# A cross-attention block on one core: scores leave PSUM two heads at a time, most maxima are finished on VectorE, and the order of all engines is written anew

## The chip, the cores and the metric

The kernel runs on one core of a Trainium2 chip. The metric is the device time of one launch in microseconds (us); lower is better. The core has five engines with queues of their own: TensorE (PE, matmuls), VectorE (DVE), ScalarE (ACT), GpSimd (POOL) and SyncE (SP, which here only issues DMAs). Each takes its instructions in order and waits for the others by semaphores. TensorE writes its results to PSUM, which has eight banks of 128 partitions x 512 fp32 numbers; the other data lie in SBUF.

## The reference

Eight batches of 256 tokens, width 512, 16 heads of 32, all in fp32:

```python
def layer_norm(x, w, b):
    mu = jnp.mean(x, axis=-1, keepdims=True)
    var = jnp.mean(jnp.square(x - mu), axis=-1, keepdims=True)
    return (x - mu) * jax.lax.rsqrt(var + EPS) * w + b
x = layer_norm(hidden_states, ln1_w, ln1_b)
q = (x @ q_w + q_b).reshape(B, LQ, H, HD).transpose(0, 2, 1, 3)
k = (encoder_hidden_states @ k_w + k_b).reshape(B, LK, H, HD).transpose(0, 2, 1, 3)
v = (encoder_hidden_states @ v_w + v_b).reshape(B, LK, H, HD).transpose(0, 2, 1, 3)
scores = jnp.einsum('bhqd,bhkd->bhqk', q, k) * scale
scores = jnp.where(mask, scores, mask_value)
attn = jax.nn.softmax(scores, axis=-1)
out = jnp.einsum('bhqk,bhkd->bhqd', attn, v)
out = out @ cproj_w + cproj_b
hidden = out + residual
y = layer_norm(hidden, ln2_w, ln2_b)
y = jax.nn.gelu(y @ fc_w + fc_b, approximate=True)
y = y @ proj_w + proj_b
return residual + y
```

The MLP's inner width is 2048. Queries and keys are 256 tokens each.

## The kernel before, in words

**Stages.** The eight batches are worked in two groups of four (g = 0, 1). For each group: the context and the normalised tokens are turned (transposed) by TensorE or VectorE; q, k and v are projected; 16 attention units follow (four heads hg by batch b, named u = g, hg, b: unit 132 is group 1, heads hg = 3, batch 2); then the output projection with the residual (o), LayerNorm, the MLP's first product (fc) with gelu, and its second (pd). Group 0's attention lies beside group 1's projections, group 1's attention beside the output projection and the first fc products.

**Projections** use Strassen's scheme in Winograd's form: a product of 2 x 2 blocks takes seven matmul groups P1 to P7 instead of eight, with sums of blocks before (names ending in s, t, i such as `fw0i`, `z1t`, `a0t`, made on VectorE or GpSimd) and after (the evictions `t1` to `t3`, `c11` to `c22`). fc and pd use it on two levels. X, Y and W name the banks that such a product holds.

**One attention unit.** Eight score matmuls (L1023; each matmul leaves two records in the profile) put keys by queries into four banks, one head a bank, two key blocks each. ScalarE moves each head and key block to SBUF, adding the mask as a bias (`ev`, L614, 128x256, eight a unit). VectorE reduces with a 32x32 transpose to maxima over 32 x 32 blocks (`mx`, L1033, two a unit). ScalarE copies three 32x64 pieces of these from partitions 32, 64 and 96 to partition 0 (`mc`, L1039); VectorE reduces over the four pieces and the two key blocks (`fold`, L1040) and transposes once (`mf`, L1042). The result goes through DRAM and comes back broadcast over all partitions (`md`, `mm`), and is subtracted from the scores (`less`, L1053 on VectorE or L1057 on GpSimd), which then go through exp (L1060). `av`: TensorE multiplies the exponentials with v, and with ones for the sums of each row; `r` and `att` (L1083 to L1086, L625) divide. Of a unit of kind "z" the two key blocks are first added (`ss`, L625), and the row sums take four matmuls; of kind "p" they are not, and take eight. `KINDS` lists the kinds.

**What sets the order.** Each piece of work is one operation with a name (`T.op`). The table `PROGRAM` lists all names in one order; an operation that can run on several engines has a letter behind its name (:A ScalarE, :V VectorE, :G GpSimd). Each engine gets its operations in that order and no scheduler changes it. The table `PLACES` gives each buffer its slot of SBUF or its PSUM bank. The framework adds the semaphore waits that follow from it. The eight banks are eight tiles of 128x512, of kind W (projections) or C (scores, av, turns). A matmul waits until the last reader of the bank's previous contents is done.

**The start.** TensorE runs 12 small matmuls on constants first (`small`, L646), and 4 more behind the first turned blocks.

## Time and profile before

| | us |
|---|---|
| median of 3 runs (lowest, highest) | 654.15 (653.59, 655.86) |
| span of the profiled execution | 652.0 |
| TensorE busy in it | 644.3 |
| VectorE / ScalarE / GpSimd busy | 583.2 / 346.1 / 395.9 |
| start of the scores of unit 000; of 031; of 100 (group 1's first) | 63.2; 158.6; 186.4 |
| first product of group 1's output projection | 367.3 |
| last matmul's end | 648.5 |

The profile is one execution; its span lies 2.15 us below the median of the runs. In the rows an operation's line is that of the helper that records it (L634 is every matmul of the projections and of attention, L614 the score evictions, L601 and L606 other evictions, L623 and L625 sums). A row's tile names are those of the tile that was first put in the slot by that name in the program, so a projection may read "xt" or "vw" where another buffer has since taken that slot.

### The profile page before, as it was taken

The page shows a single profiled execution, that of the slowest core. Times are in us where ns is not written, and L with a number is a line of the kernel's source. Part 1 is how long each engine was busy: PE and PEld are TensorE (multiplying, and loading weights), DVE is VectorE, ACT ScalarE, POOL GpSimd, SP SyncE. Part 2 cuts the span into 40 slices and gives each one's busy share as a digit, 9 for nine tenths or more (in the row PEclk, how much of TensorE's full clock was granted, in tenths as well). Part 3 has the DMA queues.
Part 4 walks back from the last instruction along what each step waited for, and adds up shares of the span by engine and source line. Part 5 has one row for each costly group of instructions (what it writes and reads, how often), then busy time and mean ns, then how long its engine had stood idle before and what let it go on. Part 6 is the DMA issues. An engine that isn't in the chain of part 4 may idle for free.

```text
span 652.0 us, 11225 instructions
## 1 busy us (share of the span) xinstructions
PE 644.3 (99%) x3793; PEld 487.7 (75%) x3793; DVE 583.2 (89%) x985; ACT 346.1 (53%) x709; POOL 395.9 (61%) x351
## 2 busy tenths in 40 slices
PE   9999999999999999999999999999999999999997
PEld 7755463477545776777787888888888888888886
DVE  4989998999999999999999999988878777999975
ACT  2244698999999879966864645220121222523000
POOL 2543675879987897898859756335813265321244
PEclk9999999999999999999999999999999999999999
DMA  8999998778875447787867787897989989677765
GB/s 268 306 328 324 239 251 284 226 204 152 217 224 151 130 168 232 260 267 250 257 214 250 225 272 232 293 314 170 160 222 197 215 198 204 158 190 227 173 138 97
DMA packets 206713, 144.83 MB, mean 222 GB/s; under 512 B 117136, under 2 KB 167104, under 8 KB 206656
## 3 DMA queue, kind: packets, MB, share of 16 engines
q1 hardware_dynamic: 206656, 144.11, 78.0%
q8 instruction: 30, 0.49, 0.3%
q14 instruction: 27, 0.22, 0.1%
HBM read 104.10 MB, written 39.98 MB: 221 GB/s over the span
## 4 chain that ended last, share of the span: by engine, by line
PE 90%; DVE 4%; ACT 2%; issue 1%; DMA 1%; POOL 1%; DVEq 0%
PE pd_X L634 15%; PE fc_X L634 15%; PE fc_W L634 7%; PE pd_W L634 7%; PE av L634 6%; PE q_X L634 4%; PE v_X L634 4%; PE fc_Y L634 4%; PE k_X L634 4%; PE pd_Y L634 4%; PE s L634 4%; PE o_X L634 2%; PE v_W L634 2%; PE k_W L634 2%; PE o_W L634 2%; DVE mx L1033 2%
## 5 line engine op out<-in xcount | busy, mean ns | idle before, releaser
L614 ACT ACTIVATE pr<-s,cols 128x256 f32<-128x256 f32 x256 | 102.9, 485 | 10.7 <-PE s L634 8.2
L1057 POOL TENSOR_TENSOR pr<-pr,mm 128x512 f32<-128x512 f32 x70 | 90.2, 1318 | 7.2 <-DMA xt<-in_x_dram 5.0
L1237 ACT ACTIVATE h<-h,cols 128x256 f32<-128x256 f32 x128 | 55.2, 499 | 61.2 <-DVE h L625 45.2
L1033 DVE TRANSPOSE_TENSOR_REDUCE mx<-pr 128x32 f32<-128x1024 f32 x64 | 76.9, 1216 | 1.5 <-ACT pr L614 1.3
L1060 ACT ACTIVATE pr<-pr 128x1024 f32<-128x1024 f32 x64 | 66.5, 1061 | 12.1 <-POOL pr L1057 9.0
L625 DVE TENSOR_TENSOR h<-fc_X,h 128x512 f32<-128x512 f32 x80 | 52.4, 675 | 5.5 <-PE fc_X L634 4.7
L625 POOL TENSOR_TENSOR ss<-pr 128x512 f32<-128x512 f32 x24 | 31.5, 1325 | 14.2 <-ACT pr L1060 11.8
L625 DVE TENSOR_TENSOR h<-fc_W,h 128x512 f32<-128x512 f32 x48 | 32.0, 677 | 5.0 <-PE fc_W L634 4.4
L1053 DVE TENSOR_TENSOR pr<-pr,mm 128x1024 f32<-128x1024 f32 x29 | 35.2, 1229 | 0.0
L1039 ACT COPY mx<-mx 32x64 f32<-32x64 f32 x96 | 23.2, 243 | 15.9 <-DVE mx L1033 14.7
L623 POOL TENSOR_TENSOR z1t<-h,z1t 128x512 f32<-128x512 f32 x6 | 8.0, 1360 | 26.1 <-PE pd_Y L634 12.3
L625 POOL TENSOR_TENSOR tq<-tq,rq 128x512 f32<-128x512 f32 x8 | 10.1, 1272 | 21.7 <-DMA rq<-hd 15.4
L634 PE MATMUL pd_X<-z0i,pl 128*128 128x256 f32 x96 | 22.5, 379 | 0.0
L634 PE MATMUL fc_W<-y1i,fl 128*128 128x256 f32 x84 | 20.7, 379 | 0.0
L625 DVE TENSOR_TENSOR h<-fc_Y,h 128x512 f32<-128x512 f32 x24 | 15.9, 672 | 5.3 <-PE fc_Y L634 5.3
L634 PE MATMUL pd_W<-z1i,pl 128*128 128x256 f32 x88 | 20.6, 379 | 0.0
L1040 DVE TENSOR_REDUCE mx<-mx 32x32 f32<-32x256 f32 x32 | 18.4, 578 | 2.2 <-ACT mx L1039 2.0
L634 PEld LDWEIGHTS pd_X<-z0i,pl 128*128 128x128 f32 x96 | 18.2, 190 | 2.5
L811 POOL TENSOR_TENSOR rs_y<-rs_y,neg_half 128x2 f32<-128x2 f32 x8 | 10.2, 1289 | 15.3 <-DMA pl<-prd 7.7
L634 PE MATMUL pd_X<-h,pl 128*128 128x256 f32 x80 | 18.9, 379 | 0.0
L601 ACT COPY h<-fc_X 128x512 f32<-128x512 f32 x16 | 9.0, 594 | 18.5 <-PE fc_X L634 15.6
L625 DVE TENSOR_TENSOR po<-pd_X,po 128x256 f32<-128x256 f32 x24 | 9.9, 414 | 9.6 <-PE pd_X L634 9.4
(574 smaller groups left out, 1857.3 us busy)
## 6 DMA issues: line engine op xcount, KB each, us to landing
pl<-prd SPq DMA_DIRECT2D x65, 256.0 KB, 3.7
mm<-md SPq DMA_DIRECT2D x32, 512.0 KB, 4.3
fl<-fcd SPq DMA_DIRECT2D x40, 256.0 KB, 4.5
...
```

Of the source, the lines that this page charges most:

```text
L601: (nc.scalar.copy if e == "ACT" else nc.vector.tensor_copy)(to(), of_())
L614: lambda e: nc.scalar.activation(to(), of_(), AF.Identity, bias=bias(), scale=1.0))
L625: E[e].tensor_tensor(to(), in0(), in1(), op)
L634: nc.tensor.matmul(o(), l(), r(), start=first, stop=True, skip_group_check=True)
L811: lambda e, rs=rs: nc.gpsimd.tensor_tensor(tile_of(rs)[:, 2:4], tile_of(rs)[:, 0:2], neg_half[:, 0:2], ALU.pow), lock=True)
L1033: T.op(f"mx{u}_{h}", [("DVE", 1.126)], [(pr[h], None)], [(mx, [h])], lambda e, h=h: nc.vector.tensor_reduce(tile_of(mx)[:, 0:64].rearrange ...
L1039: lambda e, a=a: nc.scalar.copy(tile_of(mx)[0:32, 64 * a : 64 + 64 * a], tile_of(mx)[32 * a : 32 * a + 32, 0:64]))
L1040: T.op(f"fold{u}", [("DVE", 0.38)], [(mx, [0, 1, 2, 3, 4])], [(mx, [5])], lambda e: nc.vector.tensor_reduce(tile_of(mx)[0:32, 256:288], ti ...
L1053: nc.vector.tensor_tensor(p_, p_, m_[:, None, :].to_broadcast([P, 2, 512]), ALU.subtract)
L1057: E[e].tensor_tensor(p_, p_, m_, ALU.subtract)
L1060: lambda e, h=h: nc.scalar.activation(tile_of(pr[h]), tile_of(pr[h]), AF.Exp), table="exp")
L1237: lambda e, f=f, b=b, c=c: nc.scalar.activation(at(h[f][b], c), at(h[f][b], c), AF.Gelu_apprx_tanh, bias=col(c_fcb + f * 4 + c), scale=1.0 ...
```

## The change

**Scores.** A unit's four banks become two pairs of neighbouring banks, each one tile of 128x1024 (kind "D"). One ScalarE instruction (`ew`) moves one key block of both heads of a pair: 128x512, four a unit. All banks are now tiles by pairs, also those used singly; `by_bank` tells the framework which instructions meet in which bank, so that a single bank of a pair is still waited for singly.

**Maxima.** In 21 of the 32 units (`MAXIMA` "v") ScalarE copies nothing. VectorE first reduces over the two key blocks (128x64 to 32), transposes four 32x32 blocks from partitions 0, 32, 64 and 96, and reduces over the four. In the other 11 all stays as it was.

**Other parts.** `KINDS`: four units go from "z" to "p". The 4 later warm-up matmuls use a bank of their own and now stand before the first turned block. There are 14 instead of 10 small SBUF slots. The residual's bias `xb` runs on GpSimd in two halves. `PROGRAM` and `PLACES` are replaced as a whole: beside the order this moves sums between VectorE (985 to 1029 instructions, with more of them small) and GpSimd (351 to 395); ScalarE goes from 709 instructions to 519, matmuls from 1949 to 1965.

In the diff, the two tables are left out, and so are hunks that only pass names on.

```diff
-SLOTS = {"Q": (45, 1024), "P": (36, 512), "H": (14, 256), "sm": (10, 32), "mx": (3, 352)}
-BANKS = ("W", "C")
+SLOTS = {"Q": (45, 1024), "P": (36, 512), "H": (14, 256), "sm": (14, 32), "mx": (3, 352)}
+BANKS = ("W", "C", "D")
...
-KINDS = ("zzzzzzzzzzpppppp", "ppppppppppzzzzzz")
+KINDS = ("zzpzpzpzzzpppppp", "pppppppppppzzzzz")
+MAXIMA = ("vvvvavvvvvavvvvv", "vvvvaaaaavavavaa")
...
+            elif b.kind == "D":
+                b.t = banks.tile([P, 1024], F32, tag=f"D{b.slot // 2}", name=b.name)
+                pairs[b.slot // 2] = None
             else:
-                b.t = banks.tile([P, 512], F32, tag=f"B{b.slot}", name=b.name)
+                s, k = divmod(b.slot, 2)
+                if pairs.get(s) is None:
+                    pairs[s] = banks.tile([P, 1024], F32, tag=f"D{s}", name=b.name)
+                b.t = pairs[s][:, ts(k, 512)]
...
-    first = banks.tile([P, 512], F32, tag="B0", name="first")
-
-    def small(n):
+    first = banks.tile([P, 1024], F32, tag="D0", name="first")
+
+    def small(n, t):
         for _ in range(n):
-            nc.tensor.matmul(first[:64, :64], warm, warm, start=True, stop=True, skip_group_check=True)
-    small(WARM)
...
-    def scores(g, hg, b, halves):
+    def scores(g, hg, b, halves, blocks_first):
         u, q, k, v = operands_of(g, hg, b)
-        sb = [Buf(f"s{u}_{j}", "C", 2) for j in range(4)]
+        sb = [Buf(f"s{u}_{h}", "D", 2) for h in range(2)]
         mm(f"s{u}", 1.076, [(q[0], None), (k[0], None)], [(s, None) for s in sb], [
-            (lambda kc=kc, j=j: at(sb[j], kc), lambda kc=kc, j=j: row(k, j)[:, ts(kc, P)], lambda j=j: row(q, j), True)
+            (lambda kc=kc, j=j: at(sb[j // 2], 2 * (j % 2) + kc), lambda kc=kc, j=j: row(k, j)[:, ts(kc, P)], lambda j=j: row(q, j), True)
             for kc in range(2) for j in range(4)], mode="row")
         pr = [Buf(f"pr{u}_{h}", "Q", 4) for h in range(2)]
         for kc in range(2):
-            for j in range(4):
-                copy(f"ev{u}_{j}{kc}", (pr[j // 2], [2 * kc + j % 2]), (sb[j], [kc]), lambda j=j, kc=kc: at(pr[j // 2], 2 * kc + j % 2),
-                     lambda j=j, kc=kc: at(sb[j], kc), 256, lambda kc=kc: col(2 * (4 * g + b) + kc))
+            for h in range(2):
+                two = lambda t: t.rearrange("p (j n) -> p j n", j=2)
+                copy(f"ew{u}_{h}{kc}", (pr[h], [2 * kc, 2 * kc + 1]), (sb[h], [kc]), lambda h=h, kc=kc, two=two: two(at(pr[h], 2 * kc, 2)),
+                     lambda h=h, kc=kc: tile_of(sb[h]).rearrange("p (j k n) -> p j k n", j=2, k=2)[:, :, kc], 512,
+                     lambda kc=kc: col(2 * (4 * g + b) + kc))
         mx = Buf(f"mx{u}", "mx", 7)
         for h in range(2):
             T.op(f"mx{u}_{h}", [("DVE", 1.126)], [(pr[h], None)], [(mx, [h])], lambda e, h=h: nc.vector.tensor_reduce(
                 tile_of(mx)[:, 0:64].rearrange("p (k j q) -> p k j q", k=2, j=4)[:, :, 2 * h : 2 * h + 2],
                 tile_of(pr[h]).rearrange("p (n r) -> p n r", r=32), axis=mybir.AxisListType.X,
                 op=ALU.max, apply_transpose=True))
-        for a in range(1, 4):
-            T.op(f"mc{u}_{a}", [("ACT", 0.2)], [(mx, [0, 1])], [(mx, [1 + a])],
-                 lambda e, a=a: nc.scalar.copy(tile_of(mx)[0:32, 64 * a : 64 + 64 * a], tile_of(mx)[32 * a : 32 * a + 32, 0:64]))
-        T.op(f"fold{u}", [("DVE", 0.38)], [(mx, [0, 1, 2, 3, 4])], [(mx, [5])], lambda e: nc.vector.tensor_reduce(
-            tile_of(mx)[0:32, 256:288], tile_of(mx)[0:32, 0:256].rearrange("p (m c) -> p c m", c=32), axis=mybir.AxisListType.X, op=ALU.max))
-        T.op(f"mf{u}", [("DVE", 0.1)], [(mx, [5])], [(mx, [6])], lambda e: nc.vector.transpose(tile_of(mx)[0:32, 320:352], tile_of(mx)[0:32, 256:288]))
+        def fold(e):
+            t = tile_of(mx)
+            nc.vector.tensor_reduce(t[:, 64:96], t[:, 0:64].rearrange("p (k c) -> p c k", k=2), axis=mybir.AxisListType.X, op=ALU.max)
+            for a in range(4):
+                nc.vector.transpose(t[0:32, 96 + 32 * a : 128 + 32 * a], t[32 * a : 32 * a + 32, 64:96])
+            nc.vector.tensor_reduce(t[0:32, 320:352], t[0:32, 96:224].rearrange("p (a r) -> p r a", a=4), axis=mybir.AxisListType.X, op=ALU.max)
+
+        if blocks_first:
+            T.op(f"fold{u}", [("DVE", 0.85)], [(mx, [0, 1])], [(mx, [2, 3, 4, 5, 6])], fold)
+        else:
+            for a in range(1, 4):
+                T.op(f"mc{u}_{a}", [("ACT", 0.2)], [(mx, [0, 1])], [(mx, [1 + a])],
+                     lambda e, a=a: nc.scalar.copy(tile_of(mx)[0:32, 64 * a : 64 + 64 * a], tile_of(mx)[32 * a : 32 * a + 32, 0:64]))
+            T.op(f"fold{u}", [("DVE", 0.38)], [(mx, [0, 1, 2, 3, 4])], [(mx, [5])], lambda e: nc.vector.tensor_reduce(
+                tile_of(mx)[0:32, 256:288], tile_of(mx)[0:32, 0:256].rearrange("p (m c) -> p c m", c=32), axis=mybir.AxisListType.X, op=ALU.max))
+            T.op(f"mf{u}", [("DVE", 0.1)], [(mx, [5])], [(mx, [6])], lambda e: nc.vector.transpose(tile_of(mx)[0:32, 320:352], tile_of(mx)[0:32, 256:288]))
...
-            T.op("small", [("PE", 0.1)], [], [], lambda e: small(WARM2))
+            ps = Buf("ps_small", "C")
+            T.op("small", [("PE", 0.1)], [], [(ps, None)], lambda e: small(WARM2, tile_of(ps)))
...
-                made[n] = scores(*units[n], KINDS[g][n] == "z")
+                made[n] = scores(*units[n], KINDS[g][n] == "z", MAXIMA[g][n] == "v")
...
+    def biased(e, h):
+        if e == "DVE":
+            v = tile_of(h).rearrange("p (i n) -> p i n", i=2)
+            nc.vector.tensor_tensor(v, v, cb.t[:, None, :].to_broadcast([P, 2, D]), ALU.add)
+            return
+        for i in range(2):
+            nc.gpsimd.tensor_tensor(at(h, i, 1, 512), at(h, i, 1, 512), cb.t, ALU.add)
...
+    def place(b):
+        return {("Q", b.slot // 2, h) for h in (0, 1)} if b.kind == "Q" else {("Q", b.slot // 2, b.slot % 2)} if b.kind == "P" else {(b.kind, b.slot)}
+
+    def meet(o, d):
+
+        if d in o.deps:
+            return True
+        return any(a is not b and place(a) & place(b) for a in o.bufs for b in d.bufs
+                   if a.kind in SLOTS and b.kind in SLOTS)
+
+    KNOWN = mybir.DependencyInfo(mybir.DependencyClass.Sync, mybir.DependencyReason.DATA)
+    past = {}
+
+    def by_bank(o, made):
+
+        for b in {b for b, _ in o.touched if b.kind in BANKS and b.kind != "D"}:
+            tile_of(b)
+            pair, k = pairs[b.slot // 2], b.slot % 2
+            name = pair.tensor.name
+            mine = [i for i in made if any(getattr(x, "bass_ap", None) is not None and x.bass_ap.tensor.name == name for x in list(i.ins) + list(i.outs))]
+            writes = (b, True) in o.touched
+            written, read = past.setdefault((name, k), ([], []))
+            others = [(d, j) for d, j in past.get((name, 1 - k, "all"), []) if d.eng != o.eng]
+            kept = [j for d, j in others if meet(o, d)]
+            for i in mine:
+                for d, j in written + read:
+                    if d.eng != o.eng:
+                        tc.add_manual_dep(i, j.name, KNOWN, reason="same bank")
+                for d, j in others:
+                    if d in o.deps:
+                        tc.add_manual_dep(i, j.name, KNOWN, reason="operands")
+                for e in ENGINES:
+                    if e != o.eng:
+                        tc.declare_no_dep(i, group=f"{name}_{1 - k}{e}", keep=kept, reason="the pair's other bank")
+            for i in mine:
+                tc.add_to_no_dep_group(f"{name}_{k}{o.eng}", i)
+                past.setdefault((name, k, "all"), []).append((o, i))
+            last = [(o, i) for i in mine[-(4 if o.mode in ("row", "col") else 1):]]
+            if writes:
+                past[name, k] = (last, [])
+            else:
+                read.extend((o, i) for i in mine)
...
         for o in order:
+            n = len(nc.cur_bb.bb.instructions)
             o.fn(o.eng)
+            if any(b.kind in BANKS for b in o.bufs):
+                by_bank(o, list(nc.cur_bb.bb.instructions)[n:])
```

**What moves: ScalarE, unit 132's evictions.** One of this unit's score banks was taken next by the seventh product of the first half of group 1's output projection (o_W). pr_0 and pr_1 are the unit's scores in SBUF, s_0 to s_3 its banks (s_0 and s_1 the pairs afterwards); the copies with mx are maxima of other units. Before:

```order
L614 ACTIVATE pr_1_2488<-s_2_2480,cols 128x256
L1039 COPY mx_2490<-mx_2490 32x64 x2
L614 ACTIVATE pr_1_2488<-s_2_2480,cols 128x256
L614 ACTIVATE pr_0_2506<-s_1_2478,cols 128x256
L1039 COPY mx_2490<-mx_2490 32x64
L614 ACTIVATE pr_0_2506<-s_1_2478,cols 128x256
L614 ACTIVATE pr_1_2488<-s_3_2482,cols 128x256 x2
```

Now:

```order
L1038 COPY mx_2242<-mx_2242 32x64 x2
L601 ACTIVATE pr_0_2311<-s_0_2283,cols 128x512
L601 ACTIVATE pr_1_2313<-s_1_2286,cols 128x512
L601 ACTIVATE pr_0_2311<-s_0_2283,cols 128x512
L601 ACTIVATE pr_1_2313<-s_1_2286,cols 128x512
L1038 COPY mx_2299<-mx_2299 32x64 x2
```

The copies no longer stand between the unit's evictions, and the seventh product now takes a bank whose last reader is an eviction of a projection on VectorE, one TensorE operation earlier.

**VectorE, unit 020's division.** The av bank that `att` (the last row but one before, the last now) frees was taken next by the seventh product of group 1's first k projection (k_W). rc and r are the inverse of the row sums, st and mv LayerNorm's statistics, mx a unit's maximum. Before:

```order
L1083 TENSOR_REDUCE rc_1122<-av_1079 128x8
L1085 RECIPROCAL rc_1122<-rc_1122 128x8
L1086 STREAM_TRANSPOSE r_1125<-rc_1122 128x256
L802 BN_STATS st_x_0_1129<-vw_255 128x6
L625 TENSOR_TENSOR att_10_1131<-av_1079,r_1125 128x256
L1042 STREAM_TRANSPOSE mx_1032<-mx_1032 32x32
```

Now:

```order
L1028 TENSOR_REDUCE mx_1007<-mx_1007 128x32
L1030 STREAM_TRANSPOSE mx_1007<-mx_1007 32x32 x4
L1031 TENSOR_REDUCE mx_1007<-mx_1007 32x32
L789 BN_STATS st_x_3_1082<-k_0_11_410 128x6
L1082 TENSOR_REDUCE rc_1084<-v_0_X 128x8
L1084 RECIPROCAL rc_1084<-rc_1084 128x8
L1085 STREAM_TRANSPOSE r_1087<-rc_1084 128x256
L791 BN_AGGR mv_x_3_1089<-st_x_3_1082 128x2
L612 TENSOR_TENSOR att_10_1091<-v_0_X,r_1087 128x256
```

The six instructions of a maximum stand where two stood. k_W's bank is now another one, last read by a projection's eviction that ends 5.9 us of TensorE work (by the rows before) ahead of it. (A bank of a pair carries the name of the first tile made in it: v_0_X here is an av bank.)

**GpSimd, between the scores of units 110 and 101.** The rows with pr are subtractions, a0t sums of the output projection's input, pw0i sums of weights, hid the residual with its bias. Before, the last two a0t rows stand ahead of the scores of unit 110 and the first subtraction of the block behind them:

```order
L623 TENSOR_TENSOR a0t_2304<-att_11_1281,a0t_2284 128x512 x2
L623 TENSOR_TENSOR a0t_2307<-att_11_1281,att_01_1308 128x512 x2
L1057 TENSOR_TENSOR pr_1_2041<-pr_1_2041,mm_2265 128x512 x2
L625 TENSOR_TENSOR pw0i_2207<-pw_00_2022,pw0i_2207 128x256
L625 TENSOR_TENSOR k_0_11_411<-k_0_11_411,ows_1955 128x512
L1057 TENSOR_TENSOR pr_0_2203<-pr_0_2203,mm_2363 128x512 x2
```

Now:

```order
L1416 TENSOR_TENSOR hid_0_1968<-hid_0_1968,cb 128x512 x2
L612 TENSOR_TENSOR pw0i_2091<-pw_00_1839,pw0i_2091 128x256
L612 TENSOR_TENSOR pw0i_2091<-pw_00_1839 128x256
L610 TENSOR_TENSOR a0t_2162<-att_01_1259,att_00_971 128x512 x2
L610 TENSOR_TENSOR a0t_2165<-att_11_1160,a0t_2162 128x512 x2
L610 TENSOR_TENSOR a0t_2179<-att_11_1160,att_01_1259 128x512 x2
L1056 TENSOR_TENSOR pr_1_1876<-pr_1_1876,mm_2121 128x512 x2
```

The three a0t sums now stand behind the scores of unit 110 in the program, with two weight sums ahead of them, and ten pairs of subtractions follow.

658 lines of the change are left out of this document (320 added, 338 removed).

## The prediction

> **What bounds the kernel now.** I read the page's busy times first, then its chain of waits, then the table of PE's waits, and last the windows and timelines around each wait.
>
> ```profile
> span 652.0 us, 11225 instructions
> PE 644.3 (99%) x3793; PEld 487.7 (75%) x3793; DVE 583.2 (89%) x985; ACT 346.1 (53%) x709; POOL 395.9 (61%) x351
> PE 90%; DVE 4%; ACT 2%; issue 1%; DMA 1%; POOL 1%; DVEq 0%
> PE k_W L634 <- DVE mx L1042: 1.5, 1, 1.5
> PE o_W L634 <- ACT pr L614: 1.0, 1, 1.0
> ```
>
> TensorE is busy for 644.3 of 652.0 us and makes up nine tenths of the chain that ends last. The most that an edit on another engine can give is what TensorE now waits. VectorE is next, at 89%; ScalarE, where most of this change lies, is at 53%. The two long waits are named by their releasers, and these are partly misnamed: they are waits for PSUM banks, as the timelines show.
>
> ```profile
> 109.16 0.45 DVE L1086 STREAM_TRANSPOSE r<-rc 128x256 f32<-128x256 f32 x1
> 109.75 0.69 DVE L802 BATCH_NORM_STATS2 st_x<-vw 128x6 f32<-128x512 f32 x1
> 110.36 0.41 DVE L625 TENSOR_TENSOR att<-av,r 128x256 f32<-128x256 f32 x1
> 110.91 1.95 PE L634 MATMUL k_W<-c1t,xt 128*128 128x512 f32 x4 [1.50 <-DVE mx L1042]
> ```
>
> The bank that k_W writes at 110.91 was the av bank that the instruction `att` frees at 110.36 + 0.41 = 110.77. VectorE had put a LayerNorm statistic of 0.69 us ahead of it.
>
> ```profile
> 232.40 0.50 ACT L1039 COPY mx<-mx 32x64 f32<-32x64 f32 x2 [1.19 <-DVE mx L1033]
> 232.91 0.84 ACT L614 ACTIVATE pr<-s,cols 128x256 f32<-128x256 f32 x2
> 233.76 0.24 ACT L1039 COPY mx<-mx 32x64 f32<-32x64 f32 x1
> 234.02 1.20 ACT L614 ACTIVATE pr<-s,cols 128x256 f32<-128x256 f32 x3
> 235.28 1.56 PE L634 MATMUL o_W<-xt,a0t 128*128 128x256 f32 x6 [1.01 <-ACT pr L614]
> ```
>
> Here o_W takes a bank that held scores of unit 132. ScalarE stood 1.19 us for a maximum (to copy it), and the score evictions queued behind that.
>
> To see smaller losses I took every matmul's start against the next one's, less the usual step of its shape and of a switch of tile form. Between 60 and 380 us (attention and the first MLP's start) 24 places lose 6.4 us together; the first large one is the 1.50 above (1.66 by starts), the last 0.09 at 344.89. The windows show idle time alone, which is less:
>
> ```profile
> 0.00:60.00 60.00, 59.02 (x246) 39.13 (x247) 46.96 (x83) 21.58 (x33) 26.97 (x35) 1.00 0.94 309
> 100.00:140.00 40.00, 38.50 (x248) 20.91 (x250) 35.69 (x70) 35.96 (x75) 28.40 (x23) 1.00 0.76 248
> 220.00:260.00 40.00, 38.99 (x385) 28.59 (x384) 39.57 (x80) 35.15 (x70) 33.68 (x28) 1.00 0.59 196
> 344.89 1.12 PE L634 MATMUL fc_Y<-y0t,fl 128*128 128x256 f32 x4
> 380.00:652.00 272.00, 268.50 (x1254) 235.43 (x1252) 228.29 (x366) 60.14 (x131) 114.37 (x100) 1.00 0.79 201
> ```
>
> Columns are window, length, then busy us of PE, weight load, DVE, ACT, POOL, the granted clock (1.00 throughout), and DMA. After 380 us the lost 3.50 is nearly all the last store behind the last matmul (starts give 0.6 lost before it). So what this change can win lies between 60 and 380 us, and is 6.4 us at most.
>
> **The change part by part.** *Work added to TensorE.* Four units go from "z" (key halves added beforehand, 4 sum matmuls) to "p" (8 sum matmuls): 16 matmuls more, of two records each. A unit's pair of groups, by starts:
>
> ```profile
> 166.43 0.64 PE L634 MATMUL av<-ss,ones 128*32 128x256 f32 x8
> 167.75 0.61 PE L634 MATMUL av<-ss,ones 128*32 128x256 f32 x8
> 246.94 1.05 PE L634 MATMUL av<-pr,ones 128*32 128x256 f32 x16
> 248.66 1.05 PE L634 MATMUL av<-pr,ones 128*32 128x256 f32 x16
> ```
>
> A "z" unit takes 167.75 − 166.43 = 1.32 us, a "p" unit 248.66 − 246.94 = 1.72. Four times 0.40 is +1.6 us, on the path. The warm-up adds 8 filler matmuls ahead of the first transpose:
>
> ```profile
> 0.98 2.82 PE L646 MATMUL first<-warm 128*64 128x64 f32 x24 [0.98 <-DVE warm L641]
> 3.74 1.12 PE L722 MATMUL ps_c<-ident,cq 128*128 128x128 f32 x4
> 4.78 1.12 PE L646 MATMUL first<-warm 128*64 128x64 f32 x8
> ```
>
> The 8 at 4.78 hid the eviction of the block that had been turned before them: from 4.78 to 5.83, when the first projection starts. Now they run ahead of the turn, at (3.74 − 0.98) / 24 = 0.115 each, so the turn starts 0.9 later, and the projection follows its eviction bare. By the row of the copy below, 0.594, behind a turn of some 1.0 that begins at 4.66, it starts near 6.3 to 6.5: up to +0.7. Less, if the copy of the first half starts while the second is still being turned: between 0 and +0.7. I take +0.2.
>
> *ScalarE.* 256 evictions of 128x256 become 128 of 128x512, and 63 of 96 maximum copies go.
>
> ```profile
> L614 ACT ACTIVATE pr<-s,cols 128x256 f32<-128x256 f32 x256 | 102.9, 485 | 10.7 <-PE s L634 8.2
> L606 ACT ACTIVATE k<-k_X,cols 128x512 f32<-128x512 f32 x7 | 4.8, 691 | 9.2 <-PE k_X L634 4.8 <-DVE cols L688 4.5
> L601 ACT COPY h<-fc_X 128x512 f32<-128x512 f32 x16 | 9.0, 594 | 18.5 <-PE fc_X L634 15.6 <-DMA rq<-hd 2.9
> L1039 ACT COPY mx<-mx 32x64 f32<-32x64 f32 x96 | 23.2, 243 | 15.9 <-DVE mx L1033 14.7
> ```
>
> The eviction of two heads is not in this trace. Below it is bounded by the plain copy of that size, 0.594; above by two single ones, 2 × 0.485 = 0.970. I take 0.69, the row with the same operation and bias. By the rows' means: 256 × 0.485 = 124 becomes 128 × 0.69 = 88 us (76 to 124), so −36, and the copies give −63 × 0.243 = −15. At 53% this engine is no bound: all −51 us are off the path, and pay only where ScalarE releases TensorE, as at 235.28. A cost rides with it: a score bank now comes free 0.69 after the eviction begins, not 0.48, and the two heads of one bank pair share it.
>
> *VectorE.* In 21 units the maximum is finished on VectorE: a reduce over halves, four transposes from the four groups of 32 partitions, and a reduce, in place of one reduce and one transpose.
>
> ```profile
> L1040 DVE TENSOR_REDUCE mx<-mx 32x32 f32<-32x256 f32 x32 | 18.4, 578 | 2.2 <-ACT mx L1039 2.0
> L1042 DVE STREAM_TRANSPOSE mx<-mx 32x32 f32<-32x32 f32 x32 | 5.7, 183 | 0.2
> L1053 DVE TENSOR_TENSOR pr<-pr,mm 128x1024 f32<-128x1024 f32 x29 | 35.2, 1229 | 0.0
> L625 DVE TENSOR_TENSOR ss<-pr 128x512 f32<-128x512 f32 x8 | 5.3, 678 | 0.8 <-POOL ss L625 0.6 <-ACT pr L1060 0.2
> L625 DVE TENSOR_TENSOR z1t<-h,h 128x1024 f32<-128x1024 f32 x8 | 10.5, 1321 | 0.0
> 229.81 0.30 DVE L1042 STREAM_TRANSPOSE mx<-mx 32x32 f32<-32x32 f32 x2
> ```
>
> Before it costs 0.578 + 0.183 = 0.76. Afterwards four transposes are 4 × 0.183 = 0.73, and two reduces over 64 and 128 elements a partition, each between 0 and the 0.578 of the one over 256; by the elements (192 of 256) 0.43, and with a little for the second's start 0.5. So 1.2, that is +0.45 each and 21 × 0.45 = +9.5 us (the two ends: −1 to +24). The cover is work that leaves VectorE: by the order 3 subtractions, 3 half sums (1.229 and 0.678) and, in the MLP, 12 sums of 128x1024 (about 1.3), 21 us in these alone; all told, and with the smaller sums of weights, its load between 63 and 367 us goes from 324 to 315 us when each operation is priced by its row. Without that cover 9.5 us would land on an engine that is busy 35.7 to 39.6 us of each 40.
>
> Against this part speaks a rule of the Trainium skill ("VectorE: DVE Perf Modes", section "⚠️ Two Vector instructions with no wait between them"): an instruction whose input starts in another group of 32 partitions than the last one's is held until all earlier ones have finished. The two transposes above read the same group and took 0.30 together, less than twice 0.183; four from four groups would by this rule cost their full time each. That is what the sum already takes.
>
> *GpSimd* receives those sums and goes up by some 44 us priced in the same way, from 61% busy to about 68%.
>
> *The banks.* Each bank of a pair is waited for singly, as before, so pairing alone adds no wait; scores now need two whole pairs at once. What moves is the order. At the two long waits the bank's last reader changes: k_W's new bank was freed by an eviction 5.9 us of TensorE work earlier, and o_W's not by a score eviction but by VectorE's eviction of a projection. In the orders, the TensorE operations of this stretch that have no other TensorE operation between themselves and the last thing they need fall from 80 to 47; of those behind ScalarE, from 45 to 15. I therefore take the two long waits as gone (1.66 + 1.17 = 2.8 of 6.4) and the remaining 3.6 as scaled by 47/80, 2.1; with 0.6 put back for new ones that a new order always has, 2.7 are left: −3.7 us.
>
> *Sum.* 1.6 + 0.2 − 3.7 = −1.9. The profiled execution's span is 652.0; the median of the three runs, 654.15, lies 2.15 above it, which I take over unchanged. 654.15 − 1.9 = **652.3 us**, in span 650.1.
>
> **The rivals.** *All waits go.* The bank count speaks for it and ScalarE's 51 us of new slack; against it, VectorE stays near 39 of 40 us busy and frees most banks. 654.15 + 1.8 − 6.4 = 649.6.
>
> *The waits move, and none is won* (on the path, the change doesn't do what it says): ScalarE was never the bound, VectorE carries a longer chain to each maximum, and the wait at 110.91 was VectorE's own queue order. Then only the added matmuls are left: 654.15 + 1.8 = 656.0.
>
> *GpSimd becomes the bound at the first output projection.* Its queue there:
>
> ```profile
> 213.02 2.69 POOL L623 TENSOR_TENSOR a0t<-att,att 128x512 f32<-128x512 f32 x2
> 226.93 18.36 POOL L1057 TENSOR_TENSOR pr<-pr,mm 128x512 f32<-128x512 f32 x14 [1.05 <-DMA mm<-md]
> L625 POOL TENSOR_TENSOR pw0i<-pw,pw0i 128x256 f32<-128x256 f32 x2 | 5.8, 2894 | 0.0
> 252.12 1.05 PE L634 MATMUL av<-pr,ones 128*32 128x256 f32 x16
> ```
>
> Subtractions cost 18.36/7 = 2.62 a pair. The new order puts the three sums a0t (7.5 us) behind, not ahead of, the scores of unit 110, and ten pairs of subtractions between these and the scores of 101: 38 us by rows for about 29.8 us of TensorE work. If the queue is not early when it enters (before it was 2 to 3 us ahead), the last subtraction that unit 120 needs ends near 250.6, its exponential 1.06 later, and its av, wanted at 248.7, waits some 3 us; o_0's sixth product waits for a0t too. Price 4 to 5 us with what follows, beyond the 1.8, no wait won: about 660. It decides from the point where GpSimd enters later than 2 us ahead. The rows 2894 against 0.73 for the same sum at other places show how far this engine can stretch. The Trainium skill ("GPSIMD Engine Reference", section "8. Key points") says that GpSimd shares its SBUF interfaces with VectorE and contends with VectorE instructions of two SBUF inputs, which would make such stretching likelier in the same stretch; no run here separates it.
>
> **How the numbers follow.** Forecast 652.3: 0.50. All waits go, 649.6: 0.18. Waits move, 656.0: 0.20. GpSimd bound, 660: 0.12. The range, 649.5 to 657.5, holds the first three; within it the forecast's own terms give 650 to 654.5 (fold and start at their bounds). A measurement of this kernel can tell about 0.3% from no change, 1.96 us: faster means under 652.2, slower over 656.1. The forecast lies on the first edge, so its 0.50 splits evenly; 0.25 + 0.18 is 0.43 faster. Same is the other 0.25 and 0.12 of the third case, 0.37; slower its 0.08 with 0.12, 0.20.
>
> **What would show it.** Right: the profile after has no wait of TensorE over 0.7 us between 60 and 380 us; 32 more matmul records, 3825; eviction rows 128 by about 0.69 us; ScalarE busy near 295; a fold of six instructions taking about 1.2 us; VectorE's windows not fuller than before. Wrong: evictions near 0.97, which would take 0.28 × 128 back on ScalarE; waits of av for GpSimd's subtractions around 248 us; or a wait of projections for VectorE that has the size of the old ones at another place. If the span moves by more than 4 us without TensorE's idle time moving, the pricing by TensorE's waits is wrong altogether.

## The result and the profile after

| | before | after |
|---|---|---|
| median of 4 runs on one chip, us (lowest, highest) | 654.68 (653.59, 655.86) | 675.25 (671.39, 679.05) |
| span of the profiled execution, us | 652.0 | 677.3 |

The ratio is 1.03 (95% interval 1.0251 to 1.035): the change makes the kernel about 20.6 us slower. The forecast was 652.3 and its range ended at 657.5. Measured by the fastest run of the same kernel, three of the four runs of the changed kernel in experiment 2 and one of the four of experiment 12 count as slow ones; their medians, 677.62 and 660.45, include these, so nothing below rests on those two medians alone.

The page of the changed kernel, its first lines and the shares of the chain that ended last:

```profile
span 677.3 us, 11220 instructions
PE 648.7 (96%) x3825; PEld 488.3 (72%) x3825; DVE 603.2 (89%) x1029; ACT 311.1 (46%) x525; POOL 457.7 (68%) x397
PE 67%; DVE 19%; DMA 8%; issue 2%; ACT 1%; SPq 1%; POOL 1%; DVEq 0%; ACTq 0%
```

TensorE is busy 4.4 us longer (some of it at half clock, below) and idle for 28.6 us where it was idle for 7.7; its share of the chain falls from 90% to 67%, VectorE's rises from 4% to 19%. The table of TensorE's waits (total, times, longest):

```profile
PE v_X L621 <- ACT q L593: 9.8, 1, 9.8
PE s L621 <- DVE hid L612: 2.1, 1, 2.1
PE av L621 <- DMA fl<-fcd: 1.8, 1, 1.8
PE av L709 <- ACT xn_y L809: 1.8, 1, 1.8
```

Two places make most of it. The first, in the timeline of the changed kernel (start, duration, what it waited for):

```profile
179.71 0.84 DVE L1030 STREAM_TRANSPOSE mx<-mx 32x32 f32<-32x32 f32 x4
180.59 0.37 DVE L1031 TENSOR_REDUCE mx<-mx 32x32 f32<-32x128 f32 x1
180.89 14.53 DVE L1052 TENSOR_TENSOR pr<-pr,mm 128x1024 f32<-128x1024 f32 x1
...
177.12 5.00 POOL L1056 TENSOR_TENSOR pr<-pr,mm 128x512 f32<-128x512 f32 x4
182.05 2.53 POOL L610 TENSOR_TENSOR x1t<-x,x1t 128x512 f32<-128x512 f32 x2
184.50 2.51 POOL L1416 TENSOR_TENSOR hid<-hid,cb 128x512 f32<-128x512 f32 x2
186.94 4.95 POOL L1056 TENSOR_TENSOR pr<-pr,mm 128x512 f32<-128x512 f32 x4
191.82 2.51 POOL L1416 TENSOR_TENSOR hid<-hid,cb 128x512 f32<-128x512 f32 x2
...
195.50 0.69 ACT L593 ACTIVATE q<-v_X,cols 128x512 f32<-128x512 f32 x1 [12.53 <-issue]
196.24 3.64 PE L621 MATMUL v_X<-x,qws 128*128 128x512 f32 x4 [9.79 <-ACT q L593]
```

VectorE's subtraction for the scores of unit 023 (`less023_0`) takes 14.53 us instead of 1.2, while GpSimd runs instruction behind instruction; it ends 1.1 us after GpSimd's last one. ScalarE's eviction of q writes a slot of SBUF that this subtraction reads, so it waits 12.5 us for it, and the projection waits 9.8 us for the eviction's bank. The releaser that the table names, ScalarE, is only the last link. The four matmul records at 196.24 then take 3.64 us instead of 1.88. The trace's clock record reads 0.50 from 189.36 us, in the middle of the wait, to 199.60 us, so the work runs at half the granted clock from 196.24 to 199.60 us; that costs another 1.8 us.

The second place:

```profile
245.33 16.06 POOL L1056 TENSOR_TENSOR pr<-pr,mm 128x512 f32<-128x512 f32 x13
256.24 5.19 DVE L795 TENSOR_SCALAR rs_y<-mv_y 128x2 f32<-128x2 f32 x1
261.34 0.68 DVE L612 TENSOR_TENSOR hid<-o_W,hid 128x512 f32<-128x512 f32 x1
262.07 1.15 PE L621 MATMUL s<-v,k 32*128 32x256 f32 x16 [2.14 <-DVE hid L612]
```

Here an operation on two numbers a partition takes 5.19 us; elsewhere the same form takes 0.16 at the median. Behind it stand an eviction that TensorE waits 2.1 us for, and the LayerNorm: the `xn_y` wait of 1.8 us and, since the store of hid is late and loads stand behind it on SP's queue, the `fl` wait of 1.8 us. The windows of the two stretches (as in the prediction's):

```profile
180.00:220.00 40.00, 29.28 (x216) 13.70 (x218) 39.48 (x49) 21.64 (x31) 21.56 (x18) 0.87 0.36 114
260.00:300.00 40.00, 32.96 (x361) 22.97 (x362) 36.93 (x77) 29.66 (x46) 25.80 (x26) 1.00 0.78 246
```

VectorE reads as busy for 39.48 of 40 us while it stands still: time in which an instruction is kept out counts as its duration. The groups of the changed kernel that answer to the prediction's prices:

```profile
L601 ACT ACTIVATE pr<-s,cols 128x512 f32<-128x512 f32 x128 | 80.2, 685 | 27.5 <-PE s L621 23.4
L1030 DVE STREAM_TRANSPOSE mx<-mx 32x32 f32<-32x32 f32 x84 | 16.8, 200 | 1.6
L1031 DVE TENSOR_REDUCE mx<-mx 32x32 f32<-32x128 f32 x21 | 7.7, 367 | 0.7
L1028 DVE TENSOR_REDUCE mx<-mx 128x32 f32<-128x64 f32 x21 | 4.0, 191 | 0.1
L1052 DVE TENSOR_TENSOR pr<-pr,mm x26: 1181/1218/14529, 83.4 to 390.0; 128x1024 f32<-128x1024 f32 x26
```

(The last is the view of one line: shortest, median and longest of 26 subtractions, in ns.) The eviction of two heads takes 685 ns. The fold takes 0.191 + 4 x 0.200 + 0.367 = 1.36 us, against 0.76 before.

**Where the time is lost, over eight of the kernels.** As in the prediction, each group of matmuls is counted from its start to the next one's, less the usual step of its form; this time the attention groups' own steps are held to a standard too, so that before reads 9.2 us here between 60 and 380 us, not 6.4. Span less this loss is 643 to 645 us for every kernel, so the lost time accounts for the spans; the kernels with the four more units of eight sum matmuls lie 1 to 2 us above the other two, as the 1.6 us of these would have it.

| kernel | span | lost 60 to 380 us | of it 180 to 300 us |
|---|---|---|---|
| before | 652.0 | 9.2 | 3.9 |
| after | 677.3 | 33.3 | 23.8 |
| after again (experiment 2) | 671.4 | 26.7 | 16.2 |
| a pause for GpSimd (3) | 663.5 | 18.9 | 8.3 |
| before, with the new fold (9) | 662.3 | 19.5 | 6.9 |
| (3) with less GpSimd work (10) | 660.9 | 16.9 | 7.6 |
| (3) with less VectorE work (11) | 656.0 | 11.0 | 3.5 |
| (3) with a shorter fold (12) | 655.6 | 11.8 | 4.7 |

### The profile page after: what moved, and what is told of

The parts are those of the page before. It is cut to its first block, busy times and chain, and to the rows that moved or that the text cites. A ratio compares the mean times of both kernels' runs of the same rounds, so it can differ in the third digit from the quotient of the medians.

```text
span 677.3 us, 11220 instructions
## 1 busy us (share of the span) xinstructions
PE 648.7 (96%) x3825; PEld 488.3 (72%) x3825; DVE 603.2 (89%) x1029; ACT 311.1 (46%) x525; POOL 457.7 (68%) x397
## 4 chain that ended last, share of the span: by engine, by line
PE 67%; DVE 19%; DMA 8%; issue 2%; ACT 1%; SPq 1%; POOL 1%; DVEq 0%; ACTq 0%
PE fc_W L621 26%; PE fc_X L621 13%; PE fc_Y L621 12%; PE v_X L621 6%; DVE mx L1022 5%; DVE pr L1052 4%; PE av L621 3%; DMA md<-mx 2%; DMA mm<-md 2%; DVE mx L1030 2%; PE ps_small L621 2%; PE s L621 1%; DMA fl<-fcd 1%; DVE v L612 1%; PE ps_c L621 1%
## 5 line engine op out<-in xcount | busy, mean ns | idle before, releaser
L601 ACT ACTIVATE pr<-s,cols 128x512 f32<-128x512 f32 x128 | 80.2, 685 | 27.5 <-PE s L621 23.4
L612 DVE TENSOR_TENSOR h<-fc_W,h 128x512 f32<-128x512 f32 x82 | 54.1, 672 | 7.8 <-PE fc_W L621 7.6
L1052 DVE TENSOR_TENSOR pr<-pr,mm 128x1024 f32<-128x1024 f32 x26 | 47.4, 1830 | 3.5 <-DMA mm<-md 3.3
L593 ACT ACTIVATE e<-fc_W,cols 128x256 f32<-128x256 f32 x5 | 2.4, 473 | 50.2 <-PE fc_W L621 26.7
L621 PE MATMUL fc_W<-z0i,pl 128*128 128x256 f32 x96 | 22.5, 379 | 0.0
L610 POOL TENSOR_TENSOR z1t<-h,h 128x512 f32<-128x512 f32 x10 | 18.2, 1851 | 3.9 <-issue 2.5
L1416 POOL TENSOR_TENSOR hid<-hid,cb 128x512 f32<-128x512 f32 x14 | 20.0, 1456 | 0.6 <-DMA hid<-in_x_dram 0.6
L621 PEld LDWEIGHTS fc_W<-z0i,pl 128*128 128x128 f32 x96 | 18.2, 190 | 2.5
L1030 DVE STREAM_TRANSPOSE mx<-mx 32x32 f32<-32x32 f32 x84 | 16.8, 200 | 1.6
L612 DVE TENSOR_TENSOR h<-fc_X,h 128x512 f32<-128x512 f32 x24 | 16.3, 681 | 1.6 <-PE fc_X L621 1.4
L621 PE MATMUL fc_X<-z1i,pl 128*128 128x256 f32 x72 | 16.7, 379 | 0.0
```

Source lines behind the costliest of these rows:

```text
L601: lambda e: nc.scalar.activation(to(), of_(), AF.Identity, bias=bias(), scale=1.0))
L610: nc.gpsimd.tensor_tensor(to()[:, ts(k, 512)], in0()[:, ts(k, 512)], in1()[:, ts(k, 512)], op)
L612: E[e].tensor_tensor(to(), in0(), in1(), op)
L621: nc.tensor.matmul(o(), l(), r(), start=first, stop=True, skip_group_check=True)
L1030: nc.vector.transpose(t[0:32, 96 + 32 * a : 128 + 32 * a], t[32 * a : 32 * a + 32, 64:96])
L1052: nc.vector.tensor_tensor(p_, p_, m_[:, None, :].to_broadcast([P, 2, 512]), ALU.subtract)
```

## The experiments

### 1 and 2. When is VectorE kept out? And is it the kernel, or one execution?

The first kernel does none of the computation. GpSimd runs a number of subtractions of two inputs in SBUF one behind the other; VectorE runs some reductions beside them (one input each, 1.2 us) and then one sum of two inputs in SBUF. The second is the changed kernel, unaltered.

> A kernel that leaves the whole computation out: 20 cases, in each of which GpSimd runs 22 two-input sums (128x512, 1.23 us apart in the trace of the changed kernel; 128x256 in the last four cases) without a pause, while VectorE first does 1 to 19 reductions of one input (1.2 us each) and then one instruction of two SBUF inputs (or a 128x2 scalar sum) on tiles of its own. Theory 'long run' (in the changed kernel a subtraction on VectorE took 14.53 us where 1.2 is usual, 30 us into such a run, and a 128x2 sum 5.19, 25 us in; everywhere else, up to 18 us in, VectorE got in at the end of GpSimd's current instruction): early in the run VectorE's instruction takes at most 2.5 us; from some 10 to 18 instructions on it ends 1.1 us after the last of GpSimd's 22, so it takes 27 us less its start, 5 to 12 us. Rival 'chance': whether it gets in does not depend on how long the run has lasted; long ones are scattered among early and late. Rival 'not GpSimd': none of them takes over 2.5 us.

> The changed kernel once more, unaltered. 'Long run': the same two VectorE instructions (the subtraction of unit 023's first half, near 181 us, and LayerNorm's 128x2 sum near 256 us) are long again, 8 to 15 and 3 to 6 us, and TensorE loses about 10 us near 186 us; total 671 to 679. 'Chance': the long ones are at other places or missing, and the time spreads over 655 to 680.

```python
for i in range(22): nc.gpsimd.tensor_tensor(d, d, m[:, :512], ALU.subtract)          # d: the next 128x512, m: fixed
for _ in range(f): nc.vector.tensor_reduce(r[:, :32], a.rearrange("p (n r) -> p n r", r=32), ...)
nc.vector.tensor_tensor(c, a, b, ALU.add)                                             # 128x1024, two inputs
```

Here is the timeline of the first kernel; GpSimd's instructions take 1.22 us each in it. In the first three lines the sum (L63, 1.2 us when undisturbed) stands behind 13 reductions, behind 13 and two small transposes, and behind 16 and one small transpose; in the last an operation on 128x2 numbers stands in its place behind 16 (L64):

```profile
149.93 1.88 DVE L63 TENSOR_TENSOR c<-a,b 128x1024 f32<-128x1024 f32 x1
324.88 1.40 DVE L63 TENSOR_TENSOR c<-a,b 128x1024 f32<-128x1024 f32 x1
182.72 7.57 DVE L63 TENSOR_TENSOR c<-a,b 128x1024 f32<-128x1024 f32 x1
469.89 6.77 DVE L64 TENSOR_SCALAR s<-r 128x2 f32<-128x2 f32 x1
```

Up to GpSimd's 14th instruction, 16 to 17 us into its run, the sum gets in as soon as the instruction then running ends (1.88, 1.40 us). From the 17th it is kept out until the whole run has ended: 7.57 us, and an operation on 128x2 numbers 6.77 us. With GpSimd instructions of half the width (0.69 us) it was let in behind 4 reductions but kept out for 6.16 us behind 7, about 9 us into the run, where it got in at 16.8 us into a run of the longer ones: so the time alone doesn't decide. The Trainium skill ("SBUF — State Buffer", section "🔬 SBUF: two separate sides") says that the port pair which these two engines share is a lock for a whole instruction, and the other engine is blocked until it ends. The early cases agree (1.88 us: the rest of one GpSimd instruction and the sum's own 1.2); the late ones do not: there the sum came during the 17th and lost the pair to the five after it as well, one after the other.

The changed kernel again: 677.62 us (663.83 to 684.08, four runs). The same two instructions were held, for 5.99 and 5.20 us. So the places belong to the kernel, and the length at the first differs between executions (14.53, 5.99). That is under the 8 to 15 us expected, and of the 10 us that TensorE was to lose behind the first place it lost 1.3: GpSimd's run was broken there by a wait of 0.33 us for a transfer, and VectorE got in. The fastest of the changed kernel's eight runs, 663.83 us, lies where experiment 3 lies, so in some executions the harm may be small. That this makes the runs of this kernel spread as they do was not shown, since only profiled runs have a trace.

### 3 and 4. Two ways to break GpSimd's run

```diff
+gap023_0 behind less011_0:G        # a GpSimd sum of 128x2 that reads the result of less023_0
-eps_y0_2 o0_1_P4 ... less110_1:G less120_0:G pow_y0_2
+eps_y0_2 pow_y0_2 o0_1_P4 ... less110_1:G less120_0:G
```

GpSimd now waits for the VectorE subtraction at the first place; at the second its own small `pow`, which needs the operation on 128x2, stands directly behind that one.

> The changed kernel with GpSimd made to pause at two places: a 128x2 sum on GpSimd that reads the subtracted scores of unit 023's first half, ahead of x1t4, and the power of LayerNorm's third block moved directly behind the sum it waits for. 'Long run': the two long VectorE instructions fall to at most 2.7 us each, TensorE's loss of 9.8 us near 186 us goes and with it the lower clock behind it (1.8 us), and that of 2.1 near 260: 13 to 17 us less than the changed kernel, 658 to 662. 'Not GpSimd' (the long instructions have another cause, and GpSimd's queue is merely full beside them): within 3 us of the changed kernel, since GpSimd gets no less work.

663.93 us (661.38 to 666.28), ratio to before 1.0134 (1.0083 to 1.0185): 11.3 us under the changed kernel. The timeline at the first place:

```profile
180.12 2.31 DVE L1053 TENSOR_TENSOR pr<-pr,mm 128x1024 f32<-128x1024 f32 x1
182.51 0.19 POOL L1060 TENSOR_TENSOR gap<-pr 128x2 f32<-128x2 f32 x1 [1.17 <-DVE pr L1053]
207.67 1.93 PE L621 MATMUL q_X<-pr,ones 128*32 128x256 f32 x16 [2.49 <-ACT qws L593]
```

One pause of 1.17 us on GpSimd turns 14.53 into 2.31, and both long waits are gone, as expected. That VectorE was kept out is therefore shown as the cause of some 11 us. Both places were mended in one kernel, so how the 11 us divide between them is not shown. The time itself was forecast 658 to 662 and came out above: 9 us against before remain, at other places. One is the 2.49 above. Behind it, and behind a wait of 1.93 at 323.64 us, the granted clock was 0.50 for 3.41 us each time, which costs about 1.7 us each time, some 3.4 of the 18.9 us that this kernel still loses.

The other way moves two of GpSimd's sums (`xb0_2`, `xb0_3`, two instructions each) to VectorE, which shortens the run but leaves no pause.

```diff
-xb0_2:G ... xb0_3:G
+xb0_2:V ... xb0_3:V
```

> The changed kernel with two of GpSimd's biased residuals (xb0_2 and xb0_3, 2.5 us each, both inside the 14.5 us) moved to VectorE. 'Long run': VectorE's subtraction still waits until GpSimd's run ends, which is now about 5 us earlier: 8 to 10 us instead of 14.5, TensorE's loss there 4 to 6 instead of 9.8, total 4 to 7 us less than the changed kernel. 'Chance': no fixed relation, the subtraction 1.2 to 15 us. 'Not GpSimd': 14.5 us as before, and 2.4 us more work on VectorE: 0 to 3 us more.

674.68 us (1.0302; 1.0253 to 1.035): no gain that can be told. The subtraction was still kept out for 4.79 us and the operation on 128x2 for 5.22, with the same chain of waits behind it. This missed the expectation, which was a hold of 8 to 10 us and 4 to 7 us off the time; the hold was shorter and the time no better. So taking these 5 us of work from GpSimd without a pause did not help; the pauses did.

### 5. The edge of it

The kernel of experiment 1 with other counts, a pause in the run, and a second sum.

> Again a kernel without the computation: GpSimd runs of 22 two-input sums. In the first such kernel VectorE's instruction got in when it came 16.6 us into the run of 128x512 sums (the 14th), and was kept out to the end when it came 20.4 us in (the 17th); with 128x256 sums it got in at 5.1 us (the 8th) and was kept out from 8.9 us (the 14th). 'By count' (some 14 to 16 instructions without a break): with 128x512 in up to 15 to 17 us (11 to 13 reductions ahead) and out from 18 to 19 us (15 ahead); with 128x256 in at 6.4 and 7.7 us, out at 8.9 and 10.1. 'By time' (17 to 20 us): the 128x256 cases at 8.9 and 10.1 us get in this time. A run that is made to wait for VectorE at its 12th instruction: VectorE's sum 5 to 7 instructions later gets in, at most 2.5 us (if the count begins anew) or is kept out for 5 to 8 us (if it does not). A run in which VectorE has got in once or twice before: in again, at most 2.5 us, if getting in breaks the run, else kept out.

The sum behind 11, 12 and 13 reductions; then, behind as many as kept it out, in a run in which GpSimd had paused for VectorE's memset and was at its 4th instruction since; then twice in one run, the second time at about GpSimd's 18th instruction, the first entry having been let in:

```profile
33.15 2.02 DVE L76 TENSOR_TENSOR c<-a,b 128x1024 f32<-128x1024 f32 x1
63.16 1.96 DVE L76 TENSOR_TENSOR c<-a,b 128x1024 f32<-128x1024 f32 x1
93.16 11.67 DVE L76 TENSOR_TENSOR c<-a,b 128x1024 f32<-128x1024 f32 x1
...
390.29 1.31 DVE L76 TENSOR_TENSOR c<-a,b 128x1024 f32<-128x1024 f32 x1
443.21 2.12 DVE L76 TENSOR_TENSOR c<-a,b 128x1024 f32<-128x1024 f32 x1
454.08 2.02 DVE L76 TENSOR_TENSOR c<-a,b 128x1024 f32<-128x1024 f32 x1
```

At 63.16 GpSimd is at its 13th instruction, at 93.16 at its 14th. With instructions half as long the edge lay at the 13th to 15th as well, at 8.7 to 10 us instead of 16. So it goes by the number of GpSimd instructions without a pause, not by time, and a pause, or VectorE's getting in, starts the count anew; behind a pause, VectorE's sum got in at GpSimd's 4th and, in a second case, 6th instruction (1.31 and 1.19 us). The edge is not sharp: at the same point of an instruction it came out both ways once. What in the chip counts is not shown.

### 6 to 8. What of the rest is the order, the copies, the paired eviction?

All three are experiment 3 with one thing more: (6) three operations that TensorE was seen to wait for are moved earlier or to another engine; (7) all 32 units take their maxima in the old way, with ScalarE's copies; (8) each 128x512 eviction is made as two of 128x256 again.

```diff
(6) -... q1_1_c12 behind three exp; y0i5_2 behind less111_0; ss032_0:G
    +... q1_1_c12 ahead of them;    y0i5_2 ahead of it;      ss032_0:V
(7) -MAXIMA = ("vvvvavvvvvavvvvv", "vvvvaaaaavavavaa")
    +MAXIMA = ("aaaaaaaaaaaaaaaa", "aaaaaaaaaaaaaaaa")
(8) -copy(ew, 128x512)
    +two nc.scalar.activation of 128x256 in one operation
```

> The kernel with GpSimd's two pauses, and three moves in the order: the eviction q1_1_c12 ahead of three exponentials on ScalarE, the weight sum y0i5_2 on GpSimd ahead of a pair of subtractions, and the half sum ss032_0 from GpSimd to VectorE. In the profile of the kernel with the pauses TensorE loses 2.5 us ahead of av031 and 1.7 behind it at a lower clock, 1.9 ahead of the sixth product of fc015 and 1.7 behind it, and 1.3 ahead of av032. If these losses are queue order: 5 to 9 us less than the 663.9 of that kernel, 655 to 659. If they are only where a total shortage on VectorE and GpSimd shows: they move to the next place, 661 to 665.

> The kernel with GpSimd's two pauses, with all 32 maxima finished the old way (three copies on ScalarE, a reduction and a transpose on VectorE). VectorE has 21 x (1.36 - 0.75) = 13 us less to do by the rows of the changed kernel's profile, ScalarE 21 x 3 x 0.24 = 15 us more. The prediction's reading (VectorE's longer chain is covered): within 2 us of 663.9. Rival (VectorE is short in this stretch, so its work is paid for): 3 to 8 us less, 656 to 661.

> The kernel with GpSimd's two pauses, with each 128x512 score eviction as two of 128x256 in the same place, as before the change. ScalarE has 128 x (2 x 0.485 - 0.685) = 36 us more to do. The prediction's reading (ScalarE is no bound, the 36 us are off the path): within 2 us of 663.9. Rival (the new order relies on the shorter evictions): 3 to 10 us more, 667 to 674.

(6) 664.28 us (1.0119; 1.0085 to 1.0154): nothing won, as expected if a shortage on VectorE and GpSimd only shows at the next place (661 to 665). The wait of 2.49 us fell to 1.92, the one of 1.93 went, and others of 1.74 and 1.55 us came. No half clock followed any of them, and the time was still the same. (8) 664.42 us (1.0129; 1.0099 to 1.016): the paired eviction is worth nothing that can be measured, as the prediction had it for ScalarE's work. (7) 672.71 us (1.024; 1.0203 to 1.0278), 8.8 us slower than (3): the subtraction was kept out again, 4.66 us, and more waits end with ScalarE. Both expectations, within 2 us or 3 to 8 us less, missed. The order was written for the other form, so (7) doesn't tell what the new fold costs. Hence the next ones, which change load alone.

### 9 to 12. VectorE's load, GpSimd's load

(9) is the kernel *before*, with its own order, and only the new fold in the same 21 units:

```diff
+if blocks_first:  # the 21 units
+    T.op(f"fold{u}", [("DVE", 0.85)], [(mx, [0, 1])], [(mx, [2, 3, 4, 5, 6])], fold)
```

and the 63 copies and 21 `mf` of these units taken from the table. (10) and (11) are experiment 3 with twelve subtractions left out, of GpSimd's (31 us) or of VectorE's (14.6 us). (12) is experiment 3 with one transpose and the last reduce of each new fold left out. In (10) to (12) values differ, as the expectations say.

```diff
(10) -less020_0:G less022_0:G ... less123_0:G    # twelve names
(11) -less000_1:V less020_1:V ... less132_1:V    # twelve names
(12) -    for a in range(4):
     -        nc.vector.transpose(t[0:32, 96 + 32 * a : 128 + 32 * a], t[32 * a : 32 * a + 32, 64:96])
     -    nc.vector.tensor_reduce(t[0:32, 320:352], ...)
     +    for a in (1, 2, 3):
     +        nc.vector.transpose(t[0:32, 320:352] if a == 3 else ..., t[32 * a : 32 * a + 32, 64:96])
```

> The kernel before with one part of the change alone: in the same 21 units the maximum is finished on VectorE (halves, four transposes, reduce), the 63 copies and 21 single transposes are gone, all else and the order as before. VectorE gets 21 x 0.6 = 12.6 us more, ScalarE 15 us less. Theory: VectorE has about 1 us in 40 to spare between 60 and 340 us, some 7 us in all, so part of the 12.6 shows as waits: 3 to 7 us slower than before, without any VectorE instruction kept out for several microseconds. Rival 1 (VectorE's added work is all of after_gap's 9 us): 7 to 12 slower. Rival 2 (the order alone): within 2 us of before, or faster since the wait at 235 us was for such a copy.

> after_gap (about 664 us, 9 above the kernel before) with twelve of GpSimd's subtractions between 90 and 340 us left out (the exponentials of those twelve halves take unshifted scores times 0.125, so the values differ and the work else is the same): 12 x 2.6 = 31 us less on GpSimd, nothing less on VectorE. Theory: the remaining 9 us are late work of VectorE and GpSimd, which hold each other up; with GpSimd this much freer both the waits for its sums and the stretching of VectorE's instructions shrink, and the time falls to 655 to 658 (1.6 us of added av matmuls stay). Rival 1, VectorE's own added fold work is what makes things late: 661 to 664. Rival 2, the new order of banks loses it whatever the load: 664.

> after_gap with twelve of VectorE's subtractions in the same stretch left out in the same way: 12 x 1.22 = 14.6 us less on VectorE, a little more than the six-instruction folds had added in this stretch, nothing less on GpSimd. Theory (the two engines hold each other up, GpSimd's side the heavier): 659 to 662. Rival 1, VectorE's own load: 655 to 657, more than what freeing GpSimd gives. Rival 2, the order: 664.

> after_gap (about 664 us) with the finish of the maximum in the 21 units cut from six VectorE instructions (1.36 us) to four (0.79 us, about what the kernel before spent): one of the four transposes and the last reduce are left out, and the last transpose writes what is stored. So only one head's maxima are subtracted, and all exponentials take their argument times 0.125; the values differ, every other instruction stays. VectorE loses 21 x 0.57 = 12 us, 12 of these units before 230 us. Theory (VectorE's added fold work is most of what after_gap has lost against the kernel before, 655): 655 to 659, TensorE losing some 11 us between 60 and 380 us instead of 19. Rival (the order loses it, and the twelve left-out subtractions only helped because they ended the chain to an exponential earlier): 662 to 664.

| | us, median (lowest, highest) | before beside it | ratio (95%) |
|---|---|---|---|
| (9) | 663.42 (661.98, 666.28) | 655.17 | 1.0121 (1.0085, 1.0157) |
| (10) | 662.57 (662.29, 666.96) | 655.17 | 1.0123 (1.0076, 1.0169) |
| (11) | 657.74 (655.52, 659.5) | 655.17 | 1.0033 (1.0012, 1.0054) |
| (12) | 660.45 (657.35, 668.64) | 653.79 | 1.0135 (1.0067, 1.0203) |

The new fold alone costs the kernel before 8.2 us, though ScalarE loses 15 us of copies by it. This is not the harm of experiments 1 to 5: no VectorE instruction in its trace was stretched by more than 1.2 us. The table of TensorE's waits of (9), 60 to 380 us:

```profile
PE s L636 <- DVE qws L627: 1.5, 1, 1.5
PE v_X L636 <- DVE vw L603: 1.3, 1, 1.3
PE s L636 <- DVE vws L627: 1.2, 1, 1.2
PE o_W L636 <- ACT pr L616: 0.7, 1, 0.7
PE o_X L636 <- DVE hid L627: 0.7, 1, 0.7
```

No single one is large and most are released by VectorE: its queue runs late everywhere. The windows of 60 to 380 us, of (9) and of (11):

```profile
60.00:380.00 320.00, 309.04 (x2232) 204.57 (x2231) 312.18 (x607) 237.66 (x464) 251.95 (x213) 1.00 0.71 213
```

```profile
60.00:380.00 320.00, 315.20 (x2311) 210.46 (x2310) 297.05 (x578) 223.09 (x346) 262.94 (x240) 1.00 0.73 223
```

VectorE is busy for 312.2 us of 320 in (9), and TensorE for 7.7 us less than with before's 316.75. In (11), with VectorE at 297, TensorE loses only 11.0 us, and the time is 6.2 us under (3) and 2.6 above before, about the 1.6 us of added matmuls. (Leaving a subtraction out also shortens the chain to its exponential, so (11) by itself does not separate VectorE's load from that.) Twice as much work taken from GpSimd in (10) gives 1.4 us, which the intervals can't tell from nothing. My theory for these runs had GpSimd's side as the heavier; it falls. Rival 1, VectorE's own load, is borne out by (9) and (11), and by (12) only in part. The profiled execution of (12) lost 11.8 us, as VectorE's load would have it, but it was the fastest of four: 657.35 lies within the 655 to 659 of that reading, 659.94 and 660.97 lie between it and the 662 to 664 of its rival, and 668.64 beyond both. Its ratio to before, 1.0135, cannot be told from the 1.0134 of (3). No version tried beats the kernel before.

## Why the prediction was wrong

**The step that failed first: VectorE and GpSimd priced by their rows' means.** The part on GpSimd adds "some 44 us priced in the same way, from 61% busy to about 68%". The sum then has no term for GpSimd: 1.6 + 0.2 − 3.7 puts its added work at nothing. The share came out as said (68%), but of a longer span; the busy time itself rose from 395.9 to 457.7 us, by 62 and not 44. The harm was not in the busy time, though: GpSimd's work stood in long runs without a pause, and two VectorE instructions of 1.2 and 0.16 us became 14.53 and 5.19. Undoing that alone gave 11.3 us. No row of the profile before shows it: none of the VectorE instructions that GpSimd stretched there was more than ten GpSimd instructions into a run, and each got in at the next instruction's end. Long runs as such were not new: the kernel before has runs of up to 20 GpSimd instructions too (the changed one up to 35), but no VectorE instruction with two inputs in SBUF started later than at the 12th of one. The third rival had the right engine and quoted the Trainium skill's rule on the shared interfaces, but took it for a stretching of GpSimd's own sums and placed it around 250 us, where `av` would wait. The place was near; what waited there was VectorE.

**The step that failed second: the cover.** The prediction had +9.5 us of folds on VectorE covered by sums that leave it, "324 to 315 us", and put no loss of TensorE on them. The fold costs 1.36 us, not 1.2 (the transposes 0.200 each, the last reduce 0.367), so +12.6 us. And the total did fall: VectorE is busy 304.5 us between 60 and 380 us in experiment 3, 308.0 before. Still TensorE lost 9.7 us more, of which taking VectorE work away gave back 8 in the trace and 6.2 in the medians, and the fold alone costs before 8.2. The prediction's figures were prices, not times: the stretch from 63 to 367 us has 304 us, less than either 324 or 315. A total over 320 us is no cover for work that comes in front of evictions at particular points; on an engine with 12 us to spare in 320, the added work showed as waits at about two thirds of its size in the kernel before (8.2 of 12.6). Through which waits it does so is not settled place by place: in experiment 6 they only moved.

**The waits: −3.7 forecast.** The count "from 80 to 47" of TensorE operations that stand directly behind what they need was read as slack. The two old waits did go, as the prediction said, and the 2.7 us that were to be left became 33.3 (by the count of the table above, in which the prediction's 6.4 reads 9.2). The count takes each producer at its place in an order, and says nothing of producers that are themselves late.

**What was right.** The added matmuls (1.6 us; 3825 records), the eviction at 0.69 (measured 0.685), and ScalarE's relief being off the path (experiment 8). The first projection starts at 5.69 us, before at 5.83, so the start lost nothing either of the +0.2. The size of ScalarE's relief was wrong, without harm: the sum took 256 × 0.485 = 124 us for evictions whose row has 102.9 us of busy time, since their durations overlap in the trace; that row fell to 80.2, and with the copies (23.2 to 8.0) the engine went from 346 to 311.1 us, not near 295. That four transposes from four groups of partitions would cost their full time each, as the Trainium skill's rule had it, is borne out too: four in a row took 0.84 us (the line at 179.71), not less than 4 × 0.200, where before two from the same group took 0.30, less than 2 × 0.183. The test "if the span moves by more than 4 us without TensorE's idle time moving" did not strike: the span moved with TensorE's lost time within 1.5 us, so pricing by TensorE's waits was sound, and the waits were mis-forecast.

Of the 20.6 us, about 11.3 are shown to come from the two instructions kept out, and about 1.6 are the added matmuls. That the other 7 to 8 come from VectorE's added work is argued, not shown: the fold alone costs 8.2 in the kernel before, lightening VectorE gives back 6.2 in (11), but (12), which takes out the fold's own instructions, can't be told from (3) by its ratio. What the new order by itself adds, and what the half clock adds, were not measured apart.
